# Modulations of a PixArt-style block: four chunks in four column groups, and a setup in set order

## The chip, the cores and the metric

One core of one Trainium2 chip runs the whole program in one launch. The metric is the device time of that launch in microseconds (us); less is better. All data are float32.

## The reference

The input is x (8 batches of 512 rows, 512 features), a context of 8 x 77 rows and a conditioning vector c (8 x 512). Every weight product has 512 rows in its weight. The part that this case is about is the modulation: a vector of scales and shifts for each batch, made from silu(c).

```python
# layer 0: cross-attention, both inputs modulated
ss  = silu(c) @ W_ss + b_ss                # W_ss_q, W_ss_kv: 512 x 1024
scale, bias = split(ss, 2)
xq  = (1 + scale)[:, None, :] * ln(x)       + bias[:, None, :]
xkv = (1 + scale)[:, None, :] * ln(context) + bias[:, None, :]
x   = x + attention(xq @ Wq + bq, xkv @ Wkv + bkv) @ Wp + bp
# layer 1: self-attention, cross-attention, MLP
c_proj = silu(c) @ W_mod + b_mod           # W_mod: 512 x 3072
shift_a, scale_a, gate_a, shift_m, scale_m, gate_m = split(c_proj, 6)
x = x + gate_a * (self_attention(modulate(ln(x), shift_a, scale_a)) @ W_proj + b_proj)
x = x + attention(ln(x) @ W_qc, ln(context) @ W_kvc) @ W_cproj + b_cproj
x = x + gate_m * mlp(modulate(ln(x), shift_m, scale_m))
```

So there are ten modulation units of 512 outputs each: two for the context (W_ss_kv), two for the queries (W_ss_q), six in W_mod. Each is a product of an 8 x 512 matrix with a 512 x 512 one.

## The kernel before

The kernel has four stages: cross phase x (layer 0), the self phase a, cross phase c, and the MLP m. A setup stands ahead of cross phase x. Features lie on the partitions in KC = 4 chunks of 128 for anything that is a product's stationary or moving operand.

A modulation unit (`mod_half` for the setup, `Modulation.block` for layer 1) is computed with batches on rows. `csT` holds silu(c) turned, as four chunks of 128 x 8. Four products, one for each chunk, accumulate into 8 rows of one bank (8 x 512). ACT copies these rows out, PE turns them back by four transposes of 8 x 128 into 128 x 8 columns, and VectorE (DVE) adds the bias columns into `mod_kv`, `mod_q` or `mod_l1`. The two gates (units 2 and 5 of W_mod) are not turned: DVE adds a bias row and a DMA stores them in DRAM.

In the setup, c and the context `cx` are loaded on ACT's queue, the weights on SP's queue, the bias rows on GpSimd's (POOL). A pool of five weight buffers holds them: a load that finds none free waits, in its queue, until a product has read the buffer it will take. The order in which DVE and PE work in the setup is chosen by the scheduler; there DVE has the context's statistics (L376, L377) ahead of the copy that makes `csT` (L169). PE then does: the two context units (L101, turns L109), with the turning of the bias rows (L177) between; the turning of the normalised context (L385), in two halves, each followed by a query unit; the value products (`cv_ps`, L359, 5 tiles of 4 products); the key products (`ckT_ps`, L408, 8 x 4). After a turning of the context, DVE multiplies by the scale (L389) and POOL adds the shift (L393). Values are stored to DRAM tile by tile on SP's queue (L365) and loaded again by batch (`vr`).

Within `context_x` the order of PE is that of the code (`manual_schedule(engines={ENG.PE})`); in the cross phases that of PE, DVE, ACT and POOL is. There the work is a chain of 32 softmax steps, one for each batch b and feature chunk fc. A step does the scores (L763), maxima on DVE (L782), two sets of exponentials on ACT (L793, L796), and then, into the same PSUM banks, the output products of the step before (L828), which ACT copies out (L838) before the next scores. Between scores and outputs PE is filled: with query or projection products made of seven products each (`Seven`, L507), with the turning of the next batch's rows (`ln_T`, L291), or, in the steps that `fill` names, with a unit of W_mod. A unit is a generator; it is advanced once at each of the points where one of the seven products would stand (`mm(1)`, `mm(2)`, `mm(6)`, `mm(7)`, `mm(5)`), so its four products can stand apart. Unit 0 stands in the head of cross phase x, between the query products. Units 1, 2 and 3 fill (b, fc) = (0, 1), (1, 0) and (1, 1) of phase x, units 4 and 5 fill (0, 1) and (1, 0) of phase c.

## Time and profile before

| | |
|---|---|
| median of 3 runs | 2507.59 us (2502.64 to 2514.76) |
| the profiled execution | 2506.57 us, its span 2504.8 us |
| PE busy | 2372.6 us (95%), 17813 records |
| DVE, ACT, POOL busy | 1675.0 (67%), 1169.7 (47%), 1183.4 us (47%) |
| first product of a modulation | 15.41 us |
| value products begin | 38.42 us |
| key products end | 72.45 us |
| granted TensorE clock, mean | 0.985 |

PE records are matrix products, DVE is VectorE, ACT is ScalarE, POOL is GpSimd, SP the queue that issues most DMAs; a "q" behind an engine's name is its sequencer, which waits and issues. A line of the timeline has the start, the duration, the engine, the source line, the operation, the tiles (written <- read), the shapes and, in brackets, how long the engine was idle before it and what ended that. A float32 product shows as two records. For PE's shapes, 128*32 means 128 rows and 32 columns of stationary weights. A group's line has the count, the busy time, the mean duration of one record in ns, and the idle time before it.

### The profile page before, as it was taken

Reading aid. Unit: us, or ns where it says so; the run is one execution under the profiler, and the core shown is the slowest. Engines: PE = TensorE matmul, PEld = TensorE weight load, DVE = VectorE, ACT = ScalarE, POOL = GpSimd, SP = SyncE. Lnnn points to the kernel's source line nnn. Section 1 sums busy time; section 2 is a strip of 40 time slices with the busy share of each in tenths; the row PEclk is TensorE's granted clock in tenths of the full one; section 3 lists DMA queues with packets and bytes.
Section 4 is the critical chain, followed back from the end, with each engine's and each line's share of the span. In section 5 each row is a group of like instructions: output and inputs, shape, how many; then the busy total and the mean of one; then the engine's idle time right before and its main releaser. Section 6 shows DMA issues by size and latency. Waiting matters only on the chain. (4 is left out here: it accounts for less than half of the span.)

```text
span 2504.8 us, 44398 instructions
## 1 busy us (share of the span) xinstructions
PE 2372.6 (95%) x17813; PEld 1516.7 (61%) x17813; DVE 1675.0 (67%) x2894; ACT 1169.7 (47%) x2043; POOL 1183.4 (47%) x1210
## 2 busy tenths in 40 slices
PE   7899999899999999999988999999999999999998
PEld 3567776323333333333235677777888888888887
DVE  3577784588888889887755777767555546555553
ACT  1366663577777677777643555542122121121210
POOL 2357664367786777777654585744201102102011
PEclk9999999999999999999999899999999999999999
DMA  7456656498999999999995465453101111011010
GB/s 259 144 126 134 145 72 116 97 185 170 195 192 178 201 170 195 189 178 183 199 237 144 79 115 85 72 86 97 55 18 38 38 34 38 30 43 39 21 34 26
DMA packets 126130, 291.65 MB, mean 116 GB/s; under 512 B 13540, under 2 KB 30004, under 8 KB 125796
## 3 DMA queue, kind: packets, MB, share of 16 engines
q0 software_dynamic: 59424, 176.23, 40.8%
q1 hardware_dynamic: 60559, 100.82, 12.9%
q10 hardware_dynamic: 5941, 11.76, 1.4%
q8 instruction: 140, 2.29, 0.4%
q14 instruction: 66, 0.54, 0.1%
HBM read 252.39 MB, written 61.54 MB: 125 GB/s over the span
## 5 line engine op out<-in xcount | busy, mean ns | idle before, releaser
L1667 POOL TENSOR_TENSOR res_m<-res_m,gate_m 128x256 f32<-128x256 f32 x64 | 52.2, 815 | 655.8 <-DVE res_m L1665 655.8
L1174 POOL DMA_DIRECT2D e_a<-mxd_a x256 | 250.2, 2044 | 156.6 <-DMA mxd_a<-mxT_a 147.7
L1183 ACT ACTIVATE e_a<-e_a 128x1024 f32<-128x1024 f32 x256 | 265.6, 1058 | 84.5 <-DMA e_a<-mxd_a 84.2
L1138 ACT COPY e_a<-sT_a 128x1024 f32<-128x1024 f32 x256 | 255.1, 1011 | 94.8 <-DVE mx_a L1140 46.7
L1601 ACT ACTIVATE hT<-hT,bcol 128x512 f32<-128x512 f32 x128 | 91.9, 721 | 238.6 <-DVE hT L1576 230.6
L1190 POOL TENSOR_TENSOR sum_a<-e_a,e_a 128x1024 f32<-128x1024 f32 x64 | 153.3, 2442 | 102.8 <-ACT e_a L1183 91.7
L1190 POOL TENSOR_TENSOR sum_a<-sum_a,e_a 128x1024 f32<-128x1024 f32 x64 | 171.8, 2695 | 3.7 <-ACT e_a L1183 3.7
L1140 DVE TENSOR_TENSOR mx_a<-sT_a,mx_a 128x1024 f32<-128x1024 f32 x128 | 150.7, 1216 | 30.5 <-PE sT_a L1120 28.9
L1120 PE MATMUL sT_a<-qT_a,kT_a 32*128 32x512 f32 x1024 | 151.4, 643 | 12.2 <-ACT e_a L1138 10.6
L1200 PE MATMUL o_ps_a<-e_a,v 128*32 128x512 f32 x1024 | 145.6, 611 | 9.1 <-ACT e_a L1183 8.9
L807 POOL TENSOR_TENSOR p_x<-p_x,sm_x 128x616 f32<-128x616 f32 x64 | 83.7, 1424 | 103.5 <-DVE sm_x L803 81.5
L1568 PE MATMUL q_ps_h<-x_m,w_L_xcond_W_mlp 128*128 128x256 f32 x512 | 132.3, 381 | 0.0
L1568 PE MATMUL q_ps_h<-xT_m,w_L_xcond_W_mlp 128*128 128x256 f32 x512 | 131.5, 379 | 0.0
L304 PE MATMUL q_ps_a<-xnT_a,w_L_xcond_W_qkv 128*128 128x512 f32 x256 | 124.1, 613 | 6.9 <-ACT xnT_a L1043 6.9
L807 POOL TENSOR_TENSOR p_c<-p_c,sm_c 128x616 f32<-128x616 f32 x64 | 81.8, 1364 | 99.3 <-ACT xnT_c L293 45.3
L1218 DVE RECIPROCAL rz_a<-z_ps_a 128x512 f32<-128x512 f32 x32 | 107.4, 3357 | 31.5 <-PE z_ps_a L1211 31.5
L1568 PE MATMUL q_ps_h<-x_m,w_s 128*128 128x256 f32 x512 | 122.2, 382 | 5.0 <-DVE w_s L1522 4.3
L312 PE MATMUL v_ps<-w_L_xcond_W_qkv,xnT_a 128*128 128x512 f32 x256 | 121.0, 616 | 0.0
L304 PE MATMUL k_ps_a<-xnT_a,w_L_xcond_W_qkv 128*128 128x512 f32 x256 | 120.4, 608 | 0.0
L312 PE MATMUL proj_ps_a<-w_L_xcond_W_proj,oT_a 128*128 128x512 f32 x256 | 117.9, 604 | 1.4 <-DVE oT_a L1221 1.4
L1568 PE MATMUL q_ps_y<-w_L_xcond_W_mlp,h_s 128*128 128x256 f32 x512 | 113.1, 379 | 0.0
L1568 PE MATMUL q_ps_y<-w_L_xcond_W_mlp,hT 128*128 128x256 f32 x512 | 113.1, 379 | 0.0
(419 smaller groups left out, 5287.2 us busy)
## 6 DMA issues: line engine op xcount, KB each, us to landing
e_a<-mxd_a POOLq DMA_DIRECT2D x256, 512.0 KB, 11.7
xa<-in_L_xcond_bp_dram POOLq DMA_DIRECT2D x8, 1024.0 KB, 14.7
xa<-res_x POOLq DMA_DIRECT2D x32, 256.0 KB, 5.2
xa<-res_a POOLq DMA_DIRECT2D x32, 256.0 KB, 14.4
x_c<-xa SPq DMA_DIRECT2D x8, 1024.0 KB, 6.5
w_L_xcond_W_mlp<-in_L_xcond_W_mlp_dram SPq DMA_DIRECT2D x8, 1024.0 KB, 15.5
xa<-in_L_xcond_b_cproj_dram POOLq DMA_DIRECT2D x8, 1024.0 KB, 15.6
xa<-res_c POOLq DMA_DIRECT2D x32, 256.0 KB, 5.2
```

The source lines that it names most:

```text
L304: nc.tensor.matmul(ps, lhsT=w[:, k, ts(j, P)], rhs=xT[k], start=(k == 0), stop=(k == KC - 1))
L312: nc.tensor.matmul(ps, lhsT=xT[k][:, cols], rhs=w[:, k, :], start=(k == 0), stop=(k == KC - 1))
L807: nc.gpsimd.tensor_tensor(v, v, self.sm[i].unsqueeze(3).to_broadcast([P, 2, NT, S]), ALU.mult)
L1120: nc.tensor.matmul(sc[h // 2][:, h % 2, :], lhsT=kT[ts(h, HD), ts(k, P)], rhs=qT[ts(h, HD), :], start=True, stop=True,)
L1138: nc.scalar.copy(self.e[k][i], sc[i])
L1140: nc.vector.tensor_tensor(self.mx[1 - i], sc[1 - i], self.e[0][1 - i] if k == 1 else self.mx[1 - i], ALU.max,)
L1174: nc.gpsimd.dma_start(out=self.e[k][i].rearrange("p h n -> p (h n)"), in_=self.mxd[2 * i : 2 * i + 2, :] .rearrange("h n -> (h n)").partit ...
L1183: nc.scalar.activation(self.e[k][i], self.e[k][i], AF.Exp)
L1190: engine.tensor_tensor(sum_i, self.e[0][i] if k == 1 else sum_i, self.e[k][i], ALU.add)
L1200: nc.tensor.matmul(self.po[ts(h, HD), :], lhsT=vt[:, self.fc * P + h * HD : self.fc * P + (h + 1) * HD], rhs=self.e[k][h // 2][:, h % 2, : ...
L1218: nc.vector.reciprocal(r, self.pz)
L1568: nc.tensor.matmul(self.banks[n][:, half], lhsT=lhsT, rhs=rhs, start=(k == 0), stop=(k == len(pairs) - 1),)
```

## The change

`csT` is padded with zeros to CG = 32 columns for each chunk. The four products of a unit no longer accumulate: each writes its own quarter of the bank's 128 partitions (rows 32k to 32k + 31), with 128 x 32 weights. ACT copies all 128 rows. A product with the constant `pick` (128 x 8, a one wherever the row's number modulo 32 is the column) then adds the four parts and turns them at once: four products with 128 x 128 of the copy as weights and 8 columns of `pick`. For a gate, one product with `pick` as weights adds the parts into 8 rows of 512.

In the setup, the context goes to SP's queue, ahead of the weights; the value and key weights are loaded ahead of the query units' weights; PE and DVE work in the order of the code, with `csT` ahead of the context's statistics, and four PSUM buffers instead of two. Both context units are issued one behind the other. The context's statistics move from `context_x` to the setup, and `context_x` is now in set order on DVE too. The two query units stand among the value tiles instead of among the turnings of the context. A unit of W_mod issues its four products and its copy at its first point and the products with `pick` at its third. For unit 0 the head of phase x is split: products and copy in the middle of the seven, the rest behind them.

```diff
-    csT = const.tile([P, KC, B], F32, name="csT")
+    csT = const.tile([P, KC, CG], F32, name="csT")
+    pick = const.tile([P, B], F32, name="pick")
...
-    def mod_half(u, w, bname, dst, pool, psp, tag):
-        ps = psp.tile([P, H], F32, tag=tag, name=f"mod_ps_{bname}_{u}")
+    def mod_parts(ps, w):
         for k in range(KC):
             nc.tensor.matmul(
-                ps[:B, :], lhsT=csT[:, k, :], rhs=w[:, k, :], start=(k == 0), stop=(k == KC - 1)
+                ps[ts(k, CG), :], lhsT=csT[:, k, :], rhs=w[:, k, :], start=True, stop=True
             )
-        m = pool.tile([B, H], F32, tag="mod", bufs=2, name=f"mod_{bname}_{u}")
-        mark = nc.scalar.copy(m, ps[:B, :])
+    def mod_columns(ps, m):
+        for j in range(KC):
+            nc.tensor.matmul(ps[:, ts(j, B)], lhsT=m[:, ts(j, P)], rhs=pick, start=True, stop=True)
+
+    def mod_half(u, w, bname, dst, pool, psp, tag):
+        ps = psp.tile([P, H], F32, tag=tag, name=f"mod_ps_{bname}_{u}")
+        mod_parts(ps, w)
+        m = pool.tile([P, H], F32, tag="mod", bufs=2, name=f"mod_{bname}_{u}")
+        mark = nc.scalar.copy(m, ps)
         yield
         pt = psp.tile([P, H], F32, tag=tag, name=f"modT_ps_{bname}_{u}")
-        for j in range(KC):
-            nc.tensor.transpose(pt[:, ts(j, B)], m[:, ts(j, P)], ident[:B, :B])
+        mod_columns(pt, m)
...
-        nc.scalar.dma_start(
+        nc.sync.dma_start(
             out=cx[:, : CT - 1, :],
...
+    def context_rows(cx, mv):
+        for t in range(CT):
+            n = P if t < CT - 1 else RL
+            bn = small.tile([P, 6], F32, tag="st", name=f"cst_x_{t}")
+            nc.vector.bn_stats(bn[:n], cx[:n, t, :])
+            nc.vector.bn_aggr(mv[:n, t, :], bn[:n])
...
-    with tc.tile_pool(name="setup_ps", bufs=2, space=PSUM) as spp:
+    with tc.tile_pool(name="setup_ps", bufs=4, space=PSUM) as spp, tc.manual_schedule(
+        engines={ENG.PE, ENG.DVE}
+    ):
...
+        nc.vector.memset(csT, 0.0)
+        nc.vector.tensor_reduce(
+            pick, ident.rearrange("p (g c) -> p c g", c=CG)[:, :B, :], AX.X, ALU.add
+        )
+        c_mv = small.tile([P, CT, 2], F32, tag="cmv", bufs=1, name="cmv_x")
+        nc.vector.memset(c_mv, 1.0)
...
         w_ss_kv = [load_w("L0_xcond_Wss_kv", u) for u in range(2)]
+        w_l0 = [None, load_w("L0_xcond_Wkv", 1)]
+        w_l0[0] = load_w("L0_xcond_Wkv", 0)
...
+        context_rows(cx, c_mv)
         next(halves[0])
+        next(halves[1])
...
-        w_ss_q = [load_w("L0_xcond_Wss_q", 0)]
-        w_l0 = [None, load_w("L0_xcond_Wkv", 1)]
-        w_l0[0] = load_w("L0_xcond_Wkv", 0)
-        w_ss_q.append(load_w("L0_xcond_Wss_q", 1))
+        w_ss_q = [load_w("L0_xcond_Wss_q", u) for u in range(2)]
...
-                if k % 2:
-                    mark = run(mod_half(k // 2, w_ss_q[k // 2], "L0_xcond_bss_q", mod_q, prep, ps_m, "m"))
             vd = dram.tile([R, H], F32, name="cvd_x")
+            queries_mod = [
+                mod_half(u, w_ss_q[u], "L0_xcond_bss_q", mod_q, prep, ps_m, "m") for u in range(2)
+            ]
             for t in range(CT):
                 run(values_c(
...
+                for half in queries_mod[t - 1 : t]:
+                    next(half)
+                for half in queries_mod[t - 2 : t - 1] if t > 1 else []:
+                    run(half)
...
-            g.most(lambda: run(head[0]))
+            g.most(lambda: pump(head[0], 1 if modulated else B * KC))
+            run(head[0])
...
-                for k in range(KC):
-                    nc.tensor.matmul(
-                        ps[:B, :], lhsT=csT[:, k, :], rhs=w[:, k, :], start=(k == 0), stop=(k == KC - 1)
-                    )
...
-                    yield
-                if gate is None:
+                mod_parts(ps, w)
+                self.load(*coming)
+                nc.scalar.copy(m, ps)
+                yield
+                yield
+                if gate is not None:
+                    pg = ps_m.tile([P, H], F32, tag="m", name=f"gate_ps_{u}")
+                    nc.tensor.matmul(pg[:B, :], lhsT=pick, rhs=m, start=True, stop=True)
+                    nc.vector.tensor_tensor(g, pg[:B, :], g, ALU.add)
+                    nc.sync.dma_start(out=gate, in_=g)
+                else:
                     pt = ps_m.tile([P, H], F32, tag="m", name=f"modT_ps_{u}")
-                    for j in range(KC):
-                        nc.tensor.transpose(pt[:, ts(j, B)], m[:, ts(j, P)], ident[:B, :B])
+                    mod_columns(pt, m)
...
-            with tc.manual_schedule(engines={ENG.PE}):
+            with tc.manual_schedule(engines={ENG.PE, ENG.DVE}):
```

More of the change, by code (lines that the diff above doesn't have):

```diff
@@ L25 @@
 SCALE = HD ** -0.5
+CG = 32
 RSQRT_SEED = float(0x5F3759DF)
@@ L94, in run @@
                 return stop.value
+    def mod_parts(ps, w):
+        for k in range(KC):
+            nc.tensor.matmul(
+                ps[ts(k, CG), :], lhsT=csT[:, k, :], rhs=w[:, k, :], start=True, stop=True
[3 more added lines that the diff above has]
+            nc.tensor.matmul(ps[:, ts(j, B)], lhsT=m[:, ts(j, P)], rhs=pick, start=True, stop=True)
     def mod_half(u, w, bname, dst, pool, psp, tag):
         ps = psp.tile([P, H], F32, tag=tag, name=f"mod_ps_{bname}_{u}")
-        for k in range(KC):
-            nc.tensor.matmul(
-                ps[:B, :], lhsT=csT[:, k, :], rhs=w[:, k, :], start=(k == 0), stop=(k == KC - 1)
-            )
-        m = pool.tile([B, H], F32, tag="mod", bufs=2, name=f"mod_{bname}_{u}")
-        mark = nc.scalar.copy(m, ps[:B, :])
+        mod_parts(ps, w)
+        m = pool.tile([P, H], F32, tag="mod", bufs=2, name=f"mod_{bname}_{u}")
+        mark = nc.scalar.copy(m, ps)
         yield
         pt = psp.tile([P, H], F32, tag=tag, name=f"modT_ps_{bname}_{u}")
-        for j in range(KC):
-            nc.tensor.transpose(pt[:, ts(j, B)], m[:, ts(j, P)], ident[:B, :B])
+        mod_columns(pt, m)
         bias = bias_cols(bname, KC, KC * u)
@@ L127, in load_context @@
         )
-        nc.scalar.dma_start(out=cx[:RL, CT - 1, :], in_=rows[(CT - 1) * P :, :])
+        nc.sync.dma_start(out=cx[:RL, CT - 1, :], in_=rows[(CT - 1) * P :, :])
         return cx
@@ L164, in tile_pixart_block @@
         nc.scalar.activation(cs, c_sb, AF.Silu)
+        nc.vector.memset(csT, 0.0)
+        nc.vector.tensor_reduce(
+            pick, ident.rearrange("p (g c) -> p c g", c=CG)[:, :B, :], AX.X, ALU.add
+        )
+        c_mv = small.tile([P, CT, 2], F32, tag="cmv", bufs=1, name="cmv_x")
+        nc.vector.memset(c_mv, 1.0)
         cp = spp.tile([P, H], F32, tag="ps", name="csT_ps")
@@ L168, in tile_pixart_block @@
             nc.tensor.transpose(cp[:, ts(k, B)], cs[:, ts(k, P)], ident[:B, :B])
-        nc.vector.tensor_copy(csT.rearrange("p k b -> p (k b)"), cp[:, : KC * B])
+        nc.vector.tensor_copy(csT[:, :, :B], cp[:, : KC * B].rearrange("p (k b) -> p k b", b=B))
         w_ss_kv = [load_w("L0_xcond_Wss_kv", u) for u in range(2)]
+        w_l0 = [None, load_w("L0_xcond_Wkv", 1)]
+        w_l0[0] = load_w("L0_xcond_Wkv", 0)
         halves = [
@@ L365, in values_c, with context_x @@
             nc.sync.dma_start(out=vd[t * P : t * P + n, :], in_=v[:n, :])
-        def context_x(eps, w_k, w_v, bkv, work, prep, cx):
+        def context_x(eps, w_k, w_v, bkv, work, prep, cx, mv):
             kT = work.tile([P, KC, R], F32, tag="ckT", bufs=1, name="ckT_x")
             cT = prep.tile([P, KC, R], F32, tag="cT", bufs=1, name="cT_x")
-            mv = small.tile([P, CT, 2], F32, tag="cmv", bufs=1, name="cmv_x")
-            nc.gpsimd.memset(mv, 1.0)
-            for t, n in enumerate(parts):
-                bn = small.tile([P, 6], F32, tag="st", name=f"cst_x_{t}")
-                nc.vector.bn_stats(bn[:n], cx[:n, t, :])
-                nc.vector.bn_aggr(mv[:n, t, :], bn[:n])
             y = rsqrt(mv[:, :, 1], eps, "cx", CT)
@@ L416, in context_x @@
             prep.release()
-            return kT, vd, last, mark, mv
+            return kT, vd, last
         class ContextC:
@@ L1405, in block @@
                 ps = ps_m.tile([P, H], F32, tag="m", name=f"mod_ps_{u}")
-                m = rowp.tile([B, H], F32, tag="bv", bufs=2, name=f"mod_{u}")
+                m = rowp.tile([P, H], F32, tag="bv", bufs=2, name=f"mod_{u}")
                 if gate is not None:
-                    nc.sync.dma_start(out=m, in_=a[name][ts(u, H)].partition_broadcast(B))
-                for k in range(KC):
-                    nc.tensor.matmul(
-                        ps[:B, :], lhsT=csT[:, k, :], rhs=w[:, k, :], start=(k == 0), stop=(k == KC - 1)
-                    )
-                    if k == KC - 1:
-                        self.load(*coming)
-                        if gate is None:
-                            nc.scalar.copy(m, ps[:B, :])
-                        else:
-                            nc.vector.tensor_tensor(m, ps[:B, :], m, ALU.add)
-                            nc.sync.dma_start(out=gate, in_=m)
-                    yield
-                if gate is None:
+                    g = rowp.tile([B, H], F32, tag="bv", bufs=2, name=f"gate_{u}")
+                    nc.sync.dma_start(out=g, in_=a[name][ts(u, H)].partition_broadcast(B))
+                mod_parts(ps, w)
[9 more added lines that the diff above has]
+                else:
                     pt = ps_m.tile([P, H], F32, tag="m", name=f"modT_ps_{u}")
-                    for j in range(KC):
-                        nc.tensor.transpose(pt[:, ts(j, B)], m[:, ts(j, P)], ident[:B, :B])
+                    mod_columns(pt, m)
                     bias = bias_cols(name, KC, KC * u)
@@ L1439, in tile_pixart_block @@
             names = ("L0_xcond_bq", "L0_xcond_bkv", a["L0_xcond_bp"])
-            with tc.manual_schedule(engines={ENG.PE}):
-                kT, vd, last, mark, c_mv = context_x(1e-5, w_l0[0], w_l0[1], names[1], kv_x, sp, cx)
+            with tc.manual_schedule(engines={ENG.PE, ENG.DVE}):
+                kT, vd, last = context_x(1e-5, w_l0[0], w_l0[1], names[1], kv_x, sp, cx, c_mv)
             stack.enter_context(tc.manual_schedule(engines=ALL_BUT_SYNC))
```

## The prediction

> **What bounds the kernel now.** I read the page first. PE is busy 95% of 2504.8 us; its chain that ended last runs through the last batches and says nothing of the stretch that is edited, so the rest comes from the timeline. The whole execution took 2506.57 us, 1.0 below the median of the runs shown (2507.59); the sum is made against 2506.57. First the timeline of the first 75 us:

> ```profile
> 12.79 2.47 DVE L376 BATCH_NORM_STATS2 cst_x<-cx 128x6 f32<-128x512 f32 x4 [12.79 <-DMA cx<-in_ctx_dram]
> 15.18 0.17 DVE L169 COPY csT<-csT_ps 128x32 f32<-128x32 f32 x1
> 15.41 5.31 PE L101 MATMUL od_ps_L_xcond_bss_kv<-w_L_xcond_Wss_kv,csT 128*8 128x512 f32 x8 [10.43 <-DVE csT L169]
> 27.89 3.60 PE L101 MATMUL mod_ps_L_xcond_bss_q<-w_L_xcond_Wss_q,csT 128*8 128x512 f32 x8
> 38.42 17.43 PE L359 MATMUL cv_ps_x<-w_L_xcond_Wkv,cT_x 128*128 128x512 f32 x40
> 55.70 16.75 PE L408 MATMUL ckT_ps_x<-cT_x,w_L_xcond_Wkv 128*128 128x308 f32 x64
> ```

> A product shows as two records, each 0.43 us from start to start at 512 columns. The copy of csT, a 0.17 us step, stands on DVE behind statistics that wait for the context; PE therefore does nothing useful until 15.41, and then four modulations, partly waiting for their copies and turns, before the first value product at 38.42. From there to 72.3 PE is dense. The first eight records take 5.31 us where the same eight later take 3.60: PE ran slow there. Next the groups on PE, shapes apart, for products of the new form:

> ```profile
> L1211 PE MATMUL z_ps_a<-sum_a,ones 128*32 128x512 f32 x256 | 34.1, 605 | 1.8 <-DVE res_a L1088 1.8
> L1410 PE MATMUL mod_ps<-w_L_xcond_W_mod,csT 128*8 128x512 f32 x48 | 22.6, 593 | 0.0
> L478 PE MATMUL ckT_ps_c<-cT_last,w_L_xcond_W_kvc 128*128 128x104 f32 x32 | 4.2, 275 | 0.8 <-ACT ckT_c L483 0.8
> ```

> Four 32-column products into four quarters cost 34.1/32 = 1.07 us, against 22.6/6 = 3.77 for four accumulating ones. Last, the timeline around a modulation that fills a softmax step (cross phase x, batch 1, second feature chunk), and the same step in cross phase c, which has no filling:

> ```profile
> 147.53 3.60 PE L1410 MATMUL mod_ps<-w_L_xcond_W_mod,csT 128*8 128x512 f32 x8
> 150.65 0.96 ACT L796 ACTIVATE p_x<-s_x,mx_x 128x77 f32<-128x77 f32 x4
> 151.47 0.56 ACT L1416 COPY mod<-mod_ps 8x512 f32<-8x512 f32 x1
> 151.66 1.48 PE L828 MATMUL s_x<-pw_x,vr_x 32*32 32x128 f32 x92 [0.19 <-ACT p_x L796]
> ...
> 1407.60 2.90 PE L828 MATMUL s_c<-pw_c,vr_c 32*32 32x128 f32 x96 [3.33 <-DVE pw_c L816]
> 1411.03 2.35 PE L763 MATMUL s_c<-ckT_c,qT_c 32*128 32x77 f32 x32 [0.53 <-ACT oT_c L838]
> ```

> With the filling, PE's output products still wait 0.19 us for ACT's exponentials: the filling hides completely. Without it PE stands 3.33 us and then runs at half speed, 2.90 for 1.48. The granted clock by stretch confirms it (the last three figures of a line are clock, DMA share and GB/s):

> ```profile
> 76.00:80.50 4.50, 3.63 (x12) 3.06 (x12) 1.90 (x3) 2.03 (x3) 3.87 (x3) 0.62 0.81 203
> 1408.00:1413.00 5.00, 4.37 (x128) 3.51 (x124) 2.14 (x5) 1.81 (x5) 4.92 (x5) 0.50 1.05 221
> ```

> **Setup.** The context (1.26 MB) now goes first on SP's queue. The stretches 2 to 4 and 4 to 6 us moved 276 and 402 GB/s, 1.36 MB, so it is moved by 5.8; a 256 KB store lands 2.0 us after issue, of which 0.7 is its bytes at 386 GB/s, so some 1.3 come on top: 7.1 instead of 12.8. The two Wss_kv halves follow at 2.75 us each: landed at 9.8 and 12.6. The two context DMAs leave ACT's queue, which loses nothing by it. The three new DVE steps (two clears, the sum for `pick`) and the csT copy lie in DVE's idle time before 7.

> Parts for kv: 1.07 us each, doubled at the slow start: 9.8 to 11.9 and 12.6 to 14.7. Bias columns 0.5: 15.2. Products with `pick`: eight records with 128x128 weights and 8 columns. Not in the trace; the old turns cost 0.41 for four single records, L478's short products 4.2/4 = 1.05 for eight. I take 0.9 (nearer to L478, two records a product as every product here), 1.3 while slow: 17.8. DVE now has a new wait: the second mod_kv stands ahead of four normalisations of the context (0.54 each) and the four cT products, so these begin at 18.0: 20.2. PE's turning of the context (1.28 per two sets at full clock, 1.28 per set at half) ends at 24.4, POOL's last addition (1.2 each) at 26.4, the first value tile at about 28.0. Before it ended at 38.42 + 3.43 = 41.9: 13.9 earlier. The two q modulations now stand among the value tiles: 2 x (1.07 + 0.9) = 3.9 back, their copies (0.59 at 128 rows, 0.57 at 8) beside value products. Value and key products are unchanged. **Setup: -10.0.** Bounds: PE at full clock from 18.9 as before and `pick` at 0.41 gives -13.5; `pick` bound by eight loads of 0.19 and PE slow until 29 gives -7.

> Moved on SP: Wp, x of batch 1 and the first W_mod chunk now stand behind value stores, at about 31 to 37; they are wanted after 60 by POOL and PE, so at least 20 us cover them. x of batch 0 goes out near 15 on ACT's queue instead of 25.37, and DVE has normalised it by 37.

> **The six blocks of L1's modulation.** Block 0 stands between query products that wait for nothing else: 80.89 to 85.50 is 4.6 us of parts, copy and turns. After: 1.07, and the `pick` products later, mostly in the 0.66 us in which PE waits for ACT. **-3.3.**

> Blocks 1, 3 and 4 fill a softmax step. The parts take 1.07 instead of 3.60, which gains nothing, since the exponentials end last. But ACT's copy (0.59) now stands ahead of the second set of exponentials, where it stood behind them: outputs 0.6 later. And PE then stands 2.8 us where it was filled (148.6 to 151.4: the exponentials ahead of the copy end at 150.74, the copy 0.6 later). For what that costs, the c step without filling: from scores' end to the next scores' end 9.1 us (1404.27 to 1413.38), against 7.5 with it (147.60 to 155.14): 1.6. Block 3: 0.6 + 1.6 = +2.2. In blocks 1 and 4 DVE's statistics, not PE, hold the next maxima (115.45, no idle before it; the scores ended at 113.5), which covers 1.9 of it: +0.9 each, with 2.4 if that cover is gone.

> Blocks 2 and 5 (gates) were four single products between turns of x, each turn waiting for ACT anyway (0.66 of every 1.54 us). Removing them gains nothing; the copy costs up to 0.5, the gate product (0.86) falls in a wait. With a chance of a slow stretch: +1.0 and +0.6.

> **Sum:** -10.0 - 3.3 + 2.2 + 0.9 + 0.9 + 1.0 + 0.6 = -7.7, 2498.9. All after it is shifted only.

> [...] Gaps of 2.69 and 2.74 us (before 467.23 and 419.96) were followed by half clock here. [...] L1200's eight records between full-width and row-tiled products take 1.00 us start to start (1001.43 to 1002.43), with no visible gap at either switch. [...]

> **Rivals.**
> A: the covers hold. The gaps fall across the clock's windows and stay at full clock, and the setup gets its -13.5: -13.5 - 3.3, 0.6 back for block 3's copy and 0.5 each for 2 and 5, nothing for 1 and 4: -15.2, 2491. For it: gaps of 1.65 and 1.72 (95.76, 158.79) left the clock alone. Against: 2.00 (510.99) did not.
> B, slower: the clock at the blocks. All five filled steps lose their cover as c's step did, with 0.65 more in the following step (outputs 6.15 after maxima there, 5.5 in x) and the copy: 5 x 2.9 = 14.5 - 3.3 = +11.2, against a setup of only -7: 2511. It decides once the setup gains less than 11.2 and DVE's cover in blocks 1 and 4 is absent.
> C: the groups don't run side by side. Then each block costs 3.6 as before plus the turns: setup loses 4 for kv (slow) and 5 for q, block 0 loses 2.5: -7.7 + 11.5 = +3.8, 2510. Against: L1211.

> **How the numbers follow.** What a measurement here can tell from no change is about 0.5%, 12.5 us: 2495.1 to 2520.1. Main case 2494 to 2506, chance 0.47, likeliest 2499, a tenth of it under 2495. A 0.40, 2486 to 2496. B 0.09, C 0.04. Faster 0.05 + 0.36 = 0.41; slower 0.05, a third of B and C; same 0.54. The range reaches from A's low end to B and C, which are only just left in: 2486 to 2511.

> **What would show it.** Right: csT copied before 7 us, context statistics at about 7, first value product near 24, keys ending near 62; parts at 1.07; output products 0.6 later at blocks 1, 3, 4; half clock after 3. Wrong: context landing after 9; `pick` products over 1.5; parts near 3.6; first value product after 30; or new stalls beyond 100 us, for which I see no cause.

## The result, and the profile after

| | before | after |
|---|---|---|
| median (20 runs each) | 2506.19 us | 2522.66 us |
| lowest to highest | 2497.15 to 2518.95 | 2503.07 to 2533.38 |
| ratio, 95% interval | | 1.0059 [1.0044, 1.0075] |
| profiled execution | 2506.57 | 2531.99 |
| granted clock, profiled | 0.985 | 0.978 |

The change is slower by 0.6%, 14.8 us by the ratio (the medians lie 16.5 apart); the forecast was 2499, its range 2486 to 2511. The profiled execution is one of the slowest of its kernel, 25.4 above the profiled one of before. The two traces, cut at the last key product, the last projection product of phase x, the first query product of phase c and its last projection product (the last row ends with PE's last product):

| stage, us | before | after | difference |
|---|---|---|---|
| setup, to the end of the keys | 72.4 | 60.8 | -11.6 |
| cross phase x | 357.1 | 379.6 | +22.5 |
| self phase a | 900.7 | 905.1 | +4.4 |
| cross phase c | 364.1 | 374.0 | +9.9 |
| m, the MLP | 802.5 | 802.8 | +0.3 |

The setup is a little better than forecast. The timeline of its first 61 us (start, duration, engine, line; in brackets the idle time ahead and what ended it):

```profile
4.15 0.19 DVE L196 COPY csT<-csT_ps 128x32 f32<-128x32 f32 x1 [1.44 <-PE csT_ps L195]
...
6.67 0.69 DVE L166 BATCH_NORM_STATS2 cst_x<-cx 128x6 f32<-128x512 f32 x1 [2.33 <-DMA cx<-in_ctx_dram]
...
10.54 1.94 PE L102 MATMUL od_ps_L_xcond_bss_kv<-w_L_xcond_Wss_kv,csT 128*32 128x512 f32 x8 [6.42 <-DVE cst_x L166]
...
22.05 7.68 PE L386 MATMUL cv_ps_x<-w_L_xcond_Wkv,cT_x 128*128 128x512 f32 x16
...
44.03 16.75 PE L434 MATMUL ckT_ps_x<-cT_x,w_L_xcond_Wkv 128*128 128x308 f32 x64
```

The context's statistics begin at 6.67 instead of 12.79, the first value product at 22.05 instead of 38.42, and the keys end at 60.78. The groups of the new products, shapes apart (busy us and mean ns of one, then PE's idle time ahead):

```profile
L102 PE MATMUL mod_ps<-w_L_xcond_W_mod,csT 128*32 128x512 f32 x48 | 6.5, 615 | 0.0
L109 PE MATMUL modT_ps<-pick,mod 128*128 128x8 f32 x32 | 4.9, 282 | 8.1 <-ACT mod L1439 8.1
```

The four-quarter products of six modulations now keep PE busy for 6.5 us (the accumulating ones took 22.6). But `pick`'s products wait 8.1 us for ACT's copies, 2.7 in each of blocks 1, 3 and 4. PE's timeline around block 3:

```profile
135.60 1.06 PE L102 MATMUL mod_ps<-w_L_xcond_W_mod,csT 128*32 128x512 f32 x8
139.34 1.06 PE L109 MATMUL modT_ps<-pick,mod 128*128 128x8 f32 x8 [2.67 <-ACT mod L1439]
140.33 1.90 PE L854 MATMUL s_x<-pw_x,vr_x 32*32 32x128 f32 x96
142.72 1.99 PE L789 MATMUL s_x<-ckT_x,qT_x 32*128 32x77 f32 x26 [0.50 <-ACT oT_x L864]
147.07 0.72 PE L789 MATMUL s_x<-ckT_x,qT_x 32*128 32x77 f32 x6 [2.36 <-issue]
147.72 2.07 PE L533 MATMUL sa_ps_qx<-xnT_x,w_L_xcond_Wq 128*128 128x256 f32 x4
```

The first gap was forecast, and with it the half clock that follows (96 output products take 1.90 us against 1.49). The second was not: behind 26 of 32 score products PE stands 2.36 us, and no engine or DMA that the profile names has ended it ("issue"). PE's waits by what they waited for, of the whole run (us in total, times, longest), show how much there is of this, first before, then after. L507 is `Seven`, here with projection products; L763 and L789 are scores, L854 outputs:

```profile
PE sa_ps_oc L507 <- issue: 8.0, 3, 3.6
...
PE sb_ps_ox L507 <- issue: 2.7, 1, 2.7
...
PE s_c L763 <- issue: 1.0, 1, 1.0
```

```profile
PE s_c L789 <- issue: 14.2, 4, 5.7
...
PE s_x L789 <- issue: 10.6, 6, 4.6
...
PE s_x L854 <- issue: 1.3, 1, 1.3
```

The line that I take to explain them is in the page's list of DMA queues, the same in both kernels (packets, MB, share):

```profile
q8 instruction: 140, 2.29, 0.4%
```

```
end of block   PE enters the    packet   packet   PE is through   PE goes   stand
at count       block before     begins   landed   that block      on
 5569          246.88           247.58   248.53   258.01           -        none
 6081          265.64           272.18   273.24   270.07          274.69    4.62
22209         1492.80          1502.35  1503.40  1499.21         1504.89    5.68
```

In the first row the packet begins 0.70 us after PE enters the block before, which I read as a request made at about that point, one block ahead; no trace shows the request. In the cross phases of after 10 of 81 packets begin a little earlier, at most 2.3 us before PE's first record of the block. Of the 139 packets of the run 94 begin earlier than 2 us after it (103 before). Of after's 15 and of before's 12 begin 5 to 11 us after it, and where PE needs less time than that for the block between, it stands until 1.2 to 1.6 us after the packet has landed. A step of a cross phase is 313 to 345 instructions: 128 score and output products (256 instructions), which PE runs in 2.6 us, and 28 wide ones, which take about 6.5; in one step of four 16 turnings come on top. A batch is 1286, close to five blocks, so every fifth block end falls on nearly the same work of its batch. A block lasts from 3.6 to some 11 us, by where it is cut, and the cut decides whether a late packet is noticed. The products with `pick` show as two records each where the turns showed as one. They and the other changes move the program against the blocks by 59 instructions from block 3 on, and by 71 from block 5 on.

The stands at block ends sum to 13.3 us before and 29.4 after. Each of over 2 us also goes with half clock: in the trace of after the one of 2.36 lies within a stretch of it (141.1 to 151.3), and behind those of 4.62, 5.68, 3.37 and 3.87 it stands until 281.0, 1509.8, 1554.2 and 1598.6, 6.8 us each time; before, 3.4 us from 421.7, 3.4 from 1527.6 and 6.8 from 1606.1. The windows around the longest in phase x (busy us of PE, PEld, DVE, ACT, POOL; then granted clock, DMA share, GB/s):

```profile
270.10:274.60 4.50, 0.00 (x0) 0.00 (x0) 0.00 (x0) 0.22 (x1) 4.42 (x5) 0.95 0.72 283
275.40:280.60 5.20, 5.20 (x14) 4.14 (x13) 3.75 (x6) 1.85 (x6) 0.79 (x3) 0.50 0.34 62
281.70:283.40 1.70, 1.70 (x9) 1.31 (x7) 1.51 (x4) 1.62 (x5) 1.01 (x1) 1.00 0.94 148
```

An idle PE, then 5.2 us of a full PE at half clock, then full clock. From the end of the keys to the end of phase c half clock was granted for 64.9 us before and 105.8 after. Work done at half clock took about twice its time (96 output products 2.90 us at 1407.60 of before, where 0.50 was granted, and 1.49 at full clock), so this costs at most half of the difference, 20.5. Not all of it belongs to the stands: the half clock that begins in a stand or within 2 us of its end was 13.7 us before and 47.8 after, at most 17.1 more, and another 27.3 after stand behind the gaps of blocks 1, 3 and 4. With the 16.1 more of stands this makes at most 33.2 of the 37.1 us that were lost behind the setup.

### The profile page after: what moved, and what is told of

Its sections match the earlier page's. It is cut to its first block, busy times and chain, and to the rows that moved or that the text cites. A ratio compares the mean times of both kernels' runs of the same rounds, so it can differ in the third digit from the quotient of the medians.

```text
span 2530.2 us, 44471 instructions
## 1 busy us (share of the span) xinstructions
PE 2373.0 (94%) x17849; PEld 1531.7 (61%) x17849; DVE 1681.9 (66%) x2897; ACT 1168.0 (46%) x2045; POOL 1182.5 (47%) x1209
## 5 line engine op out<-in xcount | busy, mean ns | idle before, releaser
L1147 PE MATMUL sT_a<-qT_a,kT_a 32*128 32x512 f32 x1024 | 149.2, 640 | 14.2 <-ACT e_a L1165 12.6
## 6 DMA issues: line engine op xcount, KB each, us to landing
e_a<-mxd_a POOLq DMA_DIRECT2D x256, 512.0 KB, 11.6
xa<-in_L_xcond_bp_dram POOLq DMA_DIRECT2D x8, 1024.0 KB, 15.1
```

What stands on the lines that cost most here:

```text
L1147: nc.tensor.matmul(sc[h // 2][:, h % 2, :], lhsT=kT[ts(h, HD), ts(k, P)], rhs=qT[ts(h, HD), :], start=True, stop=True,)
```

## The experiments

The theories: **A**, the place of PE's block ends, moved by added instructions, makes the loss. **B**, SP's order does (in each cross phase one load of x now stands ahead of the value loads instead of behind them). **C**, the shorter blocks' gaps and the half clock after them do. **D**, added instructions cost time in themselves, wherever they stand. All ratios are to the kernel before, run beside it on the same chip.

**Moving the block ends alone, in both kernels.**

```diff
+        pad = spp.tile([P, H], F32, tag="pad", bufs=1, name="pad_ps")
+        for i in range(30):
+            nc.tensor.transpose(pad[:, :B], ident[:B, :], ident[:B, :B])
         nc.vector.tensor_copy(csT.rearrange("p k b -> p (k b)"), cp[:, : KC * B])
```

> The kernel before, with 30 single products of 8x8 by 8x128 (60 instructions, a weight load and a product each) put on PE behind the turns of silu(c), where PE is idle until 15.4 us; nothing else is changed. In the profiled runs every long stand of PE inside a group of scores or outputs falls at an instruction count that is 193 modulo 256, and PE goes on 1.2 to 1.6 us after a 16 KB packet on the instruction queue has landed; the changed kernel has 59 instructions more ahead of batch 2 than the kernel before, so these places fall on other work. Theory A (the places where PE's instruction blocks end decide): this kernel, which shifts them alike, loses 15 to 30 us, 2520 to 2536, ratio 1.006 to 1.012, with stands of over 1 us inside scores of phase x. Theory B (the loads of x that SP now issues ahead of the value loads delay PE) and theory C (the shorter blocks leave PE idle, and the half clock that follows costs it): no change, 2506, ratio 0.999 to 1.001.

Measured: ratio **1.0141 [1.0112, 1.0170]**, more than the change itself costs and more than A's 1.006 to 1.012. The products ran from 4.84 to 8.18, in PE's idle time, and the keys ended at 73.2 (72.4 before). PE's waits of this run:

```profile
PE s_c L766 <- issue: 24.4, 6, 6.9
...
PE s_x L766 <- issue: 11.8, 4, 4.7
...
PE s_x L831 <- issue: 1.7, 1, 1.7
```

They are the waits of after: the same blocks are late by their number in the trace (7, 12, 17, 22, 23 and 36 in phase x, every fifth from 80 on in phase c), nearly all at score products. Phase x took 374.4, phase c 389.0 (379.6 and 374.0 after). Thirty tiny products in idle time, with no other part of the change, lose as much as the change loses behind its setup, with more of it in phase c.

The reverse, 98 such products in the changed kernel (`range(98)`):

> The changed kernel, with 98 such single products (196 instructions) on PE behind the turns of silu(c), which brings the ends of PE's instruction blocks to within 1 instruction (phase x) and 11 (phase c) of where they fall in the kernel before. Theory A: most of what the change lost comes back, 2494 to 2506, ratio 0.995 to 1.000, and the stands of 2.36, 4.62, 5.68, 3.37 and 3.87 us inside scores are gone. Theories B and C: as the changed kernel, 2522, ratio 1.006.

Measured: 0.9971 [0.9948, 0.9993]. Phase x came back from 379.6 to 358.8 (357.1 before) with 4.5 us of stands. Phase c did not (377.5): there the shift is 11, not 0, and four stands of 3.5 to 5.1 us had moved on to projection products. So B and C fall for phase x, where SP's order and all four blocks are still the changed ones, and A holds with a sharper edge in phase c than I had thought. The products ran until 14.4, past the weights' arrival, which cost the setup 4.7.

**Setup alone, blocks alone.** Modulation.block, the head and the tile `mod` taken from the other kernel; instructions shifted by 32, and by 27 and 39 (planned; here and below the records show the planned shift to within 2):

> The new setup alone: Modulation.block and the head are those of the kernel before, so SP's order in phases x and c is the old one and the steps keep their fillings. 32 instructions more on PE ahead of phase x and phase c. Theory A: keys end near 61 (11.5 earlier), and an unknown part of it is given back at the ends of the blocks, 2493 to 2515, ratio 0.995 to 1.004. Theories B and C: the whole gain stays, 2495, ratio 0.9955.

> The six blocks of L1's modulation changed, the setup as before (csT padded to 32 columns, of which the setup's products use 8). SP's order in phases x and c is that of the changed kernel. 27 instructions more on PE in phase x and 39 in phase c. Theory A: 2503 to 2525, by where the ends of the blocks fall. Theory B: the full loss of the changed kernel without its setup, 2534, ratio 1.011. Theory C: the same, 2530 to 2534, with half clock in blocks 1, 3 and 4 and few stands inside scores.

Measured: setup alone 1.0013 [0.9987, 1.0038], keys at 63.6, phase x 354.8, phase c 375.8 with 16.6 us of stands. Blocks alone 1.0043 [1.0024, 1.0063], phase x 359.0, phase c 384.0 with 20.9. Neither has the loss of the whole in phase x, although the second has all four blocks of that phase and SP's new order: B and C expected 1.011 there. What the setup gained, 8.9 us in this run, went in phase c, with 10.4 us of stands inside scores. The two ratios add up to nearly that of the whole change, so these two runs alone would also fit blocks that cost 0.4% in themselves; the last row of the next table decides that.

**The control, and a search.** 128 products (256 instructions) in the kernel before, 24 ahead of silu(c)'s turns and 104 behind; then the new setup alone with 60 and with 84 of them, and the whole change with 70:

> The kernel before with 128 single 8-row products on PE around the turns of silu(c): 256 instructions, one whole instruction block, so the ends of the blocks fall on the same work as in the kernel before. 128 x 0.108 us is 13.9 us at PE's first, half clock, of which some 11 lie in PE's idle time before 15.1. Theory A: the 60 instructions that cost the earlier run 1.41% did so by their place, and these 256 cost only what the setup is longer by, 2 to 4 us, ratio 0.999 to 1.004. Theory D (the added instructions themselves, their fetch or their heat, cost the time): at least as much as the 60, ratio over 1.012.

> The new setup alone with 60 such products (120 instructions): 152 instructions more than before ahead of phases x and c, a place of the block ends that no run has had. The products fit into PE's idle time, so the setup keeps its gain of about 9 to 12 us. Theory A: phase x and phase c move against the kernel before by what the stands at the block ends change by, in either direction, ratio 0.992 to 1.006, and the stands listed at the block ends account for the difference. Theory D: slower than the new setup alone (1.0013) by 0.5% or more.

> The new setup alone with 84 such products (168 instructions): 200 more than before. Worked out from the delays of the fetches that the six traces show at each place of the program, the stands at the block ends should sum to under 8 us here, against 13.3 in the kernel before and 20.2 in the new setup alone. Theory A: ratio 0.990 to 0.998, faster than both kernels. Theory D: slower than the new setup alone.

> The whole changed kernel with 70 such products (140 instructions): 199 more than before in phase x and 211 in phase c, next to the run with the new setup alone and 200. Between these two the block ends fall alike, so what is left between them is what the shorter modulation blocks themselves cost. Theory A with the forecast's working: block 0 gives 3.3 and blocks 1 to 5 cost 5.6 together, so 0 to 5 us more than its neighbour, ratio 0.991 to 1.000. Theory C (the blocks' gaps and the half clock after them make the loss): 15 to 25 us more than its neighbour, ratio over 1.002.

| kernel | shift, x / c | keys end | phase x (stands) | phase c (stands) | ratio, 95% interval |
|---|---|---|---|---|---|
| before, +256 | 256 / 256 | 74.2 | 360.8 (4.0) | 371.5 (12.6) | 1.0016 [0.9990, 1.0041] |
| setup alone, +120 | 152 / 152 | 63.6 | 379.2 (15.2) | 351.2 (1.8) | 0.9984 [0.9964, 1.0004] |
| setup alone, +168 | 200 / 200 | 64.3 | 356.8 (1.8) | 358.0 (2.4) | 0.9907 [0.9877, 0.9936] |
| whole change, +140 | 199 / 211 | 64.2 | 357.9 (2.0) | 356.9 (4.3) | **0.9907 [0.9875, 0.9939]** |

A whole block of added instructions costs nothing that can be told, a quarter of one 1.41%: D falls. The control's longest waits have their place back, at the projection products as in the kernel before:

```profile
PE sa_ps_oc L515 <- issue: 8.5, 3, 3.7
...
PE s_ps_ox L515 <- issue: 2.8, 1, 2.8
```

Shift 152 is a bad place for phase x (seven stands, one in each batch from the second) and the best here for phase c; 200 is good for both. At 152 the stands account for 11.5 of the 22.1 us that phase x loses and 7.8 of the 12.9 that phase c gains; half clock (34.1 us against 13.7, and 16.2 against 30.0) can be the rest. The changed kernel with 70 tiny products added is 0.9% faster than the kernel before, where without them it is 0.6% slower. Its neighbour with the old blocks has the same ratio, so the six blocks themselves cost nothing that these runs can tell (1.9 us between the medians, with about 11 either way), where C expected 15 to 25 more. C falls, and B with it, since SP's order is the changed one here.

**Why the packets are late.** The packet in the last row of the table above began 9.55 us after PE had entered the block before (1492.80). The timeline of all engines there:

```profile
1487.51 1.06 POOL L770 DMA_DIRECT2D xa<-in_L_xcond_b_cproj_dram  x1
...
1496.31 0.38 SPq L159 DMA_DIRECT2D x_c<-xa  x1
...
1497.72 3.03 SPq L641 DMA_DIRECT2D vr_c<-cvd_c  x4
```

POOL's transfer adds a bias row to 1 MB of residual and lands 14 to 17 us later. It goes, from both kernels:

```diff
-                if fc == 3:
-                    add_bias(b)
```

> The changed kernel without the 16 DMAs that add the output projections' bias rows to the residual (8 in phase x, 8 in phase c, 1 MB each on POOL's queue); the biases are left out of the result, and no instruction on PE, DVE, ACT or SP is changed. In phase c of the changed kernel one of them is issued at 1487.51, and the instruction block that PE asks for at 1492.80 begins to arrive only at 1502.35, while other blocks begin to arrive within 1 to 2 us. Theory E (a block that is asked for while such a transfer is under way comes late): the stands of 5.68, 3.37 and 3.87 us in phase c fall below 1 us, the sum in phase c from 15.8 to under 6, phase c from 374 to 355 to 364 us, and the whole to 2500 to 2512, ratio 0.997 to 1.002; phase x, where the loads of x, of the values and the copy of x into the residual are under way as well, gains less. Theory F (the delay is the fetch's own and does not depend on these transfers): the stands stay, 2519 to 2523, ratio 1.005 to 1.007.

> The kernel before without the same 16 DMAs, the biases left out of the result. Theory E: its stands in phase c (9.6 us) fall as well, but there is less to gain, 2496 to 2504, ratio 0.996 to 0.999, so that the distance between the two kernels shrinks from 16 us to under 8. Theory F: no change, ratio 0.999 to 1.001.

Measured: 0.9895 [0.9875, 0.9916] and 0.9882 [0.9862, 0.9902]; 2489.7 and 2487.5 us. In the changed kernel the stands of phase c are gone altogether (15.8 to 0.0; phase c 374.0 to 348.9), and what is left is in phase x:

```profile
PE s_x L789 <- issue: 4.5, 3, 3.3
...
PE sa_ps_qx L533 <- issue: 1.9, 1, 1.9
```

Of the 40 packets of phase c, 8 began over 4 us after PE's entry into the block before while the transfers were there (the latest 9.5), and one without them (4.4, ahead of the place of the first transfer). The two kernels are now 2 us apart instead of 16. F falls, and E is shown for these transfers in the changed kernel's phase c. Both kernels gained more than E expected (0.997 to 1.002 and 0.996 to 0.999). In the kernel before the stands fell from 13.3 to 1.5 us and half clock from 64.9 to 41.0, at most 24 of the 30 us gained; what the transfers cost otherwise was not taken apart. The 4.62 at the 22nd block is still 3.27, and in phase c of the kernel before two packets still began 7.9 and 6.2 us late: the loads of x and of the values, under way at these places, were not taken away one by one.

**A version with the whole result.** Each of these transfers cut in two, then both remedies together:

```diff
-                if fc == 3:
-                    add_bias(b)
+                if fc > 1:
+                    add_bias(b, fc - 2)
```

> The changed kernel with each 1 MB addition of the output projection's bias cut into two of 512 KB, one at the third and one at the fourth feature chunk of the batch; the result is complete. Theory E: each transfer lasts about half as long, so that a block which is asked for meanwhile comes at most half as late: the stands in phase c fall from 15.8 us to 3 to 10, phase x stays within 6 us of the changed kernel (its late blocks go with the loads of x and of the values, and the third chunk is where the value loads stand), 2500 to 2520, ratio 0.995 to 1.004. If the second half meets the value loads instead, nothing is gained: 1.004 to 1.008.

> The same with the 70 single products that bring the block ends to 199 and 211: both remedies together. The stands sum to 6.3 us with the products alone, so there is little left to gain: 2482 to 2497, ratio 0.987 to 0.993, within 8 us of the run with the products alone (0.9907).

Measured: the split alone 0.9944 [0.9923, 0.9966], stands 5.3 in phase x and 2.2 in phase c (13.6 and 15.8), the changed kernel's block ends untouched. That is a little more than the 0.995 to 1.004 that was expected, because phase x, at 362.2, fell by 17 us and not by up to 6. With the 70 products 0.9899 [0.9870, 0.9928]: no stand at a block end is left in either phase, which take 351.7 and 348.5. Both beat both kernels; the last is the fastest here with the whole result, level with the products alone within its interval.

## Why the prediction was wrong, step by step

- **What bounds the setup; context first.** Right. Statistics at 6.67 (forecast 7.1), first value product 22.05 (24), keys 60.8 (62). A unit's four products 1.06 to 1.19 as taken from L1211's row (1.94 and 1.86 at the slow start), `pick`'s eight records 0.95 to 1.06 (0.9 taken). The term was -10.0 and measured -11.6; with the same setup and no products added it was -8.9, -8.8 and -10.8 in three other runs. A unit between full-width products takes 0.99 from start to start (29.67 to 30.66 of after), as L1200's eight records did before (1.00): no cost of the switch between the two shapes shows.
- **Block 0.** The head start came (1.12 us for 4.61), but the next wait grew from 0.66 on ACT to 1.24 on DVE and half clock fell on 76.2 to 79.6. From the block's start to the query products behind the first scores it is 10.70 against 11.23: -0.5 of the -3.3.
- **Blocks 1 and 4.** To the second set of scores behind the block 18.64 against 19.87, and 17.60 against 18.80: -1.2 each where +0.9 stood. DVE's statistics covered the gap: the 3.48 us wait that used to follow shrank to 0.39 and 0.56. The half clock that went with that wait came earlier, and lasted 3.4 us longer each time.
- **Blocks 2 and 5.** 6.17 against 6.17, and 5.80 against 6.17: the +1.0 and +0.6 were too dear. The turns' wait for ACT in block 2 is 0.87 of every 1.53 us; the 0.66 that was read as the wait is the turn itself.
- **Block 3.** From the modulation's start to the query products 12.12 against 7.55: +4.6, of which 2.36 is the stand at a block end. The rest, +2.2, is the forecast's figure; without a stand there (whole change, +140) it was 10.54, +3.0.
- **The clock.** The gaps of 2.69, 2.67 and 2.69 us in blocks 1, 3 and 4 were each followed by half clock (96.7 to 106.9, 141.1 to 151.3, 1383.5 to 1390.3). Gaps of about 2.7 us did cost clock, as the rows of 467.23 and 419.96 had it. The windows that A speaks of show in both traces: but for the end of the run, every stretch of half clock lasted 3.41 us or two, three or four times that (3.41 from 421.7, 6.83 from 466.0 and 13.65 from 1404.7 of before, 10.24 from 96.7 of after). The gap of 2.00 at 510.99 that stood against A was misread: the granted clock is full from 511.0 to 517.2, and the eight records are two full-speed runs of four with a short hole between.
- **"All after it is shifted only".** This is the step that failed. Setup and blocks by their own terms make some -12; behind them stood a zero, and it measured +37 in the profiled run: block ends that moved by 59 to 71 instructions on to score products, 16 us more of stands and up to 17 more of half clock with them. None of the three rivals had it. B and C had the sign for other reasons: B by gaps of which all but block 3's turned out covered, C by products that don't run side by side, which at 1.06 us for four, against 3.77 for the accumulating ones, they do. "New stalls beyond 100 us" stood among the signs of being wrong, without a cause, and that sign came.

The row was there before the change: "issue" waits of 8.0 and 2.7 us on projection products of a kernel whose changed stages I had counted in microseconds and never in instructions. The 2.74 us gap before 419.96, which the prediction uses for the clock, is one of them, at count 10689; I asked what followed it and not what made it. In the kernel before with the 30 products single stands reached 6.9 us, and its "issue" waits at scores and outputs 37.9. From the nearest rows the term for the stands could have been bounded: all 13.3 us of stands gone on the one side, one of 3 to 5 us in each of the 16 batches (an estimate of 48 to 80) on the other.

Left open: whether the spread between runs (2503 to 2533 for the changed kernel) is these stands meeting transfers that land at other times; only profiled runs show stands. And what the late packets wait for within the DMA system is not visible in the trace; that they are late while a large transfer is under way, and in the changed kernel's phase c no longer when the bias transfers are gone, is all that is shown.

## What to carry to other kernels

Where PE's waits list "issue" in the middle of a group, number PE's records: if the gaps are multiples of 256 apart, as all those of over 0.9 us were here, look at how far an edit upstream moves them against the work (59 and 71 instructions here). Before judging such an edit by its time, run it once more with a few dozen tiny products added in idle time; a change of 1% by that alone (1.41% here) says that the place was measured, and not the edit. What helped here without moving the block ends was to take 1 MB transfers away from phases in which PE ran through 256 instructions in as little as 3.6 us (from 1.0059 to 0.9895, with the biases left out of the result), or to cut them in two there (0.9944).

## What the hardware showed that I had not expected

- In the trace of after the packet that I pair with PE's next block of 256 instructions began 0.99 us (the median) after PE's first record of the present one, at the earliest 4.8 us before it (2.3 in the cross phases) and at the latest 9.55 after it. Where PE had to wait, it went on 1.2 to 1.6 us after the packet had landed; the packet itself took 1.0 us (the median; 0.9 to 2.8).
- 60 instructions in idle time cost 1.41% and 256 cost 0.16% [-0.10, 0.41].
- One 1 MB accumulating transfer in each batch of the cross phases cost the kernel before 30 us (0.9882 of 2517) and the changed one some 41 (from 1.0059 to 0.9895); cutting each in two gave 29 of the 41 back (0.9944). In the chain that ended last in the kernel before, only the last of them shows (5.12 us from 1674.12).
- A weight load with its 8-row, 8-column product takes 0.108 us at the start of the run (98 in 10.60 us). PE's records ran at half speed there (1.06 us for one of 512 columns, 0.6 later), and the traces have a granted clock only from 14.8 us (after) and 18.9 us (before) on.
